# Hybrid vision block on one core: last states and the product with C on GpSimd, matmuls of an item ahead of the previous item's eviction, u * D summed in the turn

## The chip, the cores and the metric

The kernel runs on one core of a Trainium2 chip as a single launch. The core has five engines with a queue of instructions each: TensorE (PE, matrix products into PSUM; its weight loads are shown apart as PEld), VectorE (DVE), ScalarE (ACT), GpSimd (POOL) and SyncE (SP, which here only issues transfers). Each engine works through its own queue in order; an instruction that waits for another engine holds up all that stands behind it in its queue. The metric is the time of one execution on the device in microseconds (us), less is better. Device times given are medians of several runs; profiles are of one execution.

## The reference

Four images of 96 channels and 64 x 64 pixels go through four layers. Shortened to what is computed:

```python
# layer 0: x + conv(group_norm(x)); K=4 directions, N=16 states, DI=192 channels, L=4096 positions
u = silu(conv3x3_depthwise(Win @ gn(x)) + conv_b)              # b, 192, 64, 64
xs = [u by rows, u by columns, u by rows backwards, u by columns backwards]
dts, Bs, Cs = split(sel_w @ xs)                                # 6, 16, 16 rows for each direction
delta = softplus(dt_w @ dts + dt_b);  A = -exp(A_logs)
for t in range(L):                                             # a scan along the image
    h = h * exp(delta[t] * A) + (delta[t] * u[t]) * B[t]       # h: b, K, 192, 16
    y[t] = sum over the 16 states of h * C[t]
y = y + Ds * xs                                                # u * D
y = y0 + turned(y1) + y2 + turned(y3)                          # back to rows, summed
x = x + Wout @ layer_norm(y)
# layer 1: x + 1x1 conv to 576, relu, 3x3 depthwise conv, relu, 1x1 conv back to 96
# layer 2: t + ifft(relu(fft(relu(bn(W1 t))) * diag)) W2, then a feed-forward in quantised steps
# layer 3: t + linear attention (q k^T v without softmax), then a feed-forward
```

## The kernel before

**The scan and its slots.** The recurrence is the backbone. For each of the four images, four directions and eight chunks of 512 positions (128 steps in all) there are 12 units, and each unit takes one slot of the loop at L1228: 1536 slots. A unit holds 64 channels times 4 states as two halves of 128 partitions x 512. For each unit, `inputs` (L1141) makes db = (delta * u) * B for both halves at once on POOL, `decays` (L1145) makes exp(delta * A) on ACT into two PSUM banks, and `states` (L1155) runs two `tensor_tensor_scan` on DVE. In seven of the twelve units DVE also multiplies the states with C (L1166, result `hc`); in the other five, numbers 1, 3, 6, 8 and 10 (`POOL_C`), the scan writes to `hc` in SBUF and `product` (L1180) multiplies in place on POOL. `sums` (L1191) adds over the states with four small matmuls for two units, into bank `ps_y` (the trace has two records for each f32 matmul, so its counts on PE are twice those of the code); after the last pair of a group ACT copies the bank out (L1210).

**The state that is carried over.** `keep` (L1166 to L1178) saves the last column of every scan for the next chunk. For DVE's units ACT copies it from PSUM half by half (L1176); for POOL's units ACT copies both halves from `hc` (L1178), and since `product` overwrites `hc`, POOL waits for that copy.

**Order within a slot.** At slot s the loop issues: db of unit s+2, the kept states of unit s-1 together with the decays of unit s+1, POOL's product of unit s-1, the scans of unit s, the sums that are due, and then background work. The buffers `db` are three and `hc` five, the banks of decays four. Two units' sums fall due at the slot given at L1188: three slots after a POOL unit, two after another, the later of the two.

**Background.** All other layers are generators (streams) that yield before every piece of work the engine, an estimated time and the PSUM banks they need. Stages hold streams; `advance` (L1315) takes the next piece that fits from the streams of the first stage, `fits` (L1305) decides: a piece that depends on the stream's last piece on another engine is put in the same slot only after a PE piece, and only while this slot's PE estimate is at most 2.6 us; `ind` marks pieces that may go at once. `SHARE` caps each engine's background per slot, `rate` (L1238) the total. Stages run in the order of `plan` (L1076): front of images 1 and 2 (input convolution, delta, B, C), then for each image `turn` (L587: y of the two column directions is turned and added by PE), the convolutional layer, two `spectral` halves, `layer_2`, `layer_3`. Image 3's `turn` and convolution run as far as they get in the last eight steps, and the rest of image 3 runs alone after the scan, where all eight banks are used and every engine's queue is free of scan work. Three banks serve the background during the scan.

**Where u * D is added.** `scan_outputs` (L612) loads for each chunk u, the turned sum, y0 and y2, and adds them on PE: four matmuls for the first 128 channels (L638) and three, on stacked rows, for the rest (L649).

**The scheduler.** From slot 0 to the end of the scan the order of every engine is the order in which the code issues (L1351).

Of the kernel before, what the change touches and what calls it, by code (L numbers as in the profile page):

```python
# [10 lines left out]

# [16 lines left out]
L = H * W  # L28
# [22 lines left out]
WORK = {"weights": 47.0, "turn": 40.0, "front": 417.0, "conv": 468.0,  # L51
        "spectral": 111.2, "layer_2": 231.0, "product": 1.2, "layer_3": 153.6}
# [40 lines left out]
def hybrid_kernel(ctx: ExitStack, tc: tile.TileContext, a: dict):  # L93
# [347 lines left out]


# [95 lines left out]
    def scan_inputs(b, u, o, c, done):  # L538

        i = b % 3  # L540
        while not done.issuperset([c] if o == 0 else range(NCH)):
            yield wait(1)
# [12 lines left out]
        for part in range(3):  # L555
# [24 lines left out]
            yield ac(0.6, 0, True)  # L580
# [6 lines left out]
    def turn(b):  # L587
# [5 lines left out]
        for lo in (0, 128):  # L593
            for t, k in zip(parts, (1, 3)):
                load(t[:, :L].rearrange("p (c l) -> p c l", c=NCH),
                     d_y[k][im][:, lo : lo + 128, :].rearrange("c p l -> p c l"))
            yield wait(10)
            m, weights = (128, const("ident")) if lo == 0 else (64, const("two")[:, :64])
            for c in reversed(range(NCH)):
                yield pe(1.9, 1, True)  # L600
                p = bank()[:m]
                for n, t in enumerate(parts):
                    rhs = t[:, :L].rearrange("p (w h) -> p h w", h=H)[:, c * RPC : (c + 1) * RPC, :]
                    mm(split(p), lhsT=weights, rhs=rhs, start=n == 0, stop=n == 1)
                yield ac(0.6)
                s = tmp("yrow")[:m]
                nc.scalar.copy(s, p)
                free()
                later(d_yt[im][c][lo : lo + m], s)
            yield wait(2)  # L610

    def scan_outputs(b, done):  # L612

        parts = lambda c: [of[c] for of in (d_skip[b], d_yt[b % 2], d_y[0][b % 2], d_y[2][b % 2])]
        there = lambda c: scanned[b] >= 4 * NCH - c

        def fetch(*of):
            s = arrival("ypart")
            at = 0
            for x in of:  # L620
                load(s[at : at + x.shape[0]], x)
                at += x.shape[0]
            return s

        coming = None
        for c in reversed(range(NCH)):
            while not there(c):
                yield wait(1)
            if coming is None:
                coming = [fetch(of[:128]) for of in parts(c)]  # L630
                yield wait(3)
            whole, coming = coming, None
            yield pe(1.8, 1)
            p = bank()
            for n in range(4):
                if n == 2:
                    yield pe(1.8)
                mm(p, lhsT=const("ident") if n else skips[:, 0], rhs=whole[n], start=n == 0, stop=n == 3)  # L638
            yield ac(0.6)
            y = [tmp("yrow")]  # L640
            nc.scalar.copy(y[0], p)
            free()
            skip, yt, y0, y2 = parts(c)
            stacked = [fetch(skip[128:], yt[128:]), fetch(y0[128:]), fetch(y2[128:])]
            yield wait(2)
            yield pe(2.7, 1)
            p = bank()
            for n, s in enumerate(stacked):
                mm(p, lhsT=const("two") if n else skips[:, 1], rhs=s, start=n == 0, stop=n == 2)  # L649
            yield ac(0.6)  # L650
            y.append(tmp("yrow"))
            nc.scalar.copy(y[1], p)
            free()
            x = tmp("xc")
            load(x[:C], a["x"][b][:, chunk(c)])
            if c > 0 and there(c - 1):
                coming = [fetch(of[:128]) for of in parts(c - 1)]
# [36 lines left out]
    def conv_block(b):  # L694
# [6 lines left out]
        held = {}  # L701
        quads = [list(range(q, min(q + 4, NG))) for q in range(0, NG, 4)]
        slot = 0
# [14 lines left out]
        def hidden(xin, g, ready):  # L718
            nonlocal slot
            yield pe(0.9, 1, True)  # L720
            p = bank()
            for r in range(4):
                mm(p[32 * r : 32 * r + 32], lhsT=w1[:, 32 * g : 32 * g + 32], rhs=xin[:, r : r + 15 : 2, 1 : W + 1],  # L723
                   start=True, stop=True)
            yield ac(0.6)
            h = held["ring"][:, slot % 8]
            slot += 1
            act(h[:, :, 1 : W + 1], split(p), AF.Relu)
            free()
            ready.append(h)  # L730

        def rows(c):
            at = 6 * NG * 32
            xin = held["w"][:, at : at + 18 * (W + 2)].rearrange("p (r w) -> p r w", r=18)
            load(xin, d_x1[im][:, 16 * c : 16 * c + 18, :])
            yield wait(3)
            h2, ready = [], []
            for g in quads[0]:
                yield from hidden(xin, g, ready)
            for q, groups in enumerate(quads):  # L740
                coming = list(quads[q + 1]) if q + 1 < len(quads) else []
                here, ready = ready, []

                for out in ((0, 1) if len(groups) == 4 else (0,)):
                    where = [(i, out) for i in range(4)] if len(groups) == 4 else [(i, o) for o in (0, 1) for i in (0, 1)]
                    yield pe(2.7, 1, out > 0)
                    p = bank()
                    for dx in range(3):
                        for n, (i, o) in enumerate(where):
                            mm(p[32 * n : 32 * n + 32], lhsT=held["wd"][:, groups[i], o, dx, :],  # L750
                               rhs=here[i][:, :, dx : dx + W], start=dx == 0, stop=dx == 2)
                    yield ac(0.8)
# [4 lines left out]
                    for _ in range(2):  # L757
                        if coming:
                            yield from hidden(xin, coming.pop(0), ready)
            o = [tmp("o"), tmp("o")]  # L760
            for out in (0, 1):
# [14 lines left out]
                free()  # L776
            for half in (0, 1):
# [3 lines left out]
        done, to_norm = set(), []  # L781

        def blocks():
            yield from memory()
            for c in reversed(range(NCH // 2)):

                while max(2 * c - 1, 0) not in done:
# [717 lines left out]
```

## Time and profile before

| what | value |
|---|---|
| device time, median of 3 runs (lowest to highest) | 6944.3 us (6935.59 to 6944.92) |
| the profiled execution's own time, and its span | 6934.24 us, 6932.2 us |
| PE busy in the span | 4869.8 us (70%) |
| DVE busy | 5524.9 us (80%) |
| ACT busy | 4424.2 us (64%) |
| POOL busy | 5075.7 us (73%) |
| db on POOL (L1143) | 1536 of 2362 ns |
| product with C on POOL (L1181) | 640 of 2359 ns |
| decays on ACT (L1153) | 3072 of 691 ns |
| scans on DVE (L1162, four forms) | 3072 of 1204 to 1280 ns |
| product with C on DVE (L1166) | 1792 of 692 ns |
| kept state on ACT, DVE's units (L1176) / POOL's units (L1178) | 1568 of 157 ns / 560 of 185 ns |
| sums on PE (L1202) | 6144 records of 749 ns |
| transfers | 1121.47 MB, mean 162 GB/s |

The first scan starts at about 94 us and POOL's and PE's last scan work ends at about 6288 us; so the span falls into a short front, the scan, and a tail of 644 us. Read busy shares inside these stretches, not over the span: in the tail POOL has nothing to do. A waiting line is written "engine, what waited <- what it waited for"; the numbers behind it are us in total, how often, and the longest one.

### The profile page before, as it was taken

The numbers are of one execution on the slowest core, as the hardware profiler recorded it, in microseconds if no ns is written. First come the engines' busy times: TensorE is split into PE (matmuls) and PEld (weight loads), VectorE is DVE, ScalarE is ACT, GpSimd is POOL, SyncE is SP. The second block draws the span as 40 slices with busy tenths as digits, with TensorE's granted clock in tenths as the row PEclk, the third lists the DMA queues.
The fourth block names the chain that finished last, engine by engine and source line by source line (L and its number), as shares of the span: only waits on it lengthen the run. The fifth ranks groups of instructions, "written<-read, shape, count | busy, mean of one in ns | idle before, by whom it ended". The sixth has DMA issues, their size and how long they took to land. (4 is left out here: it accounts for less than half of the span.)

```text
span 6932.2 us, 85231 instructions
## 1 busy us (share of the span) xinstructions
PE 4869.8 (70%) x27820; PEld 1849.4 (27%) x27820; DVE 5524.9 (80%) x5803; ACT 4424.2 (64%) x8856; POOL 5075.7 (73%) x2183
## 2 busy tenths in 40 slices
PE   6623757656887766674688767666887676669986
PEld 2101212111224521220123353211234531112362
DVE  5979898888899889879899978998899788982110
ACT  5734776754576678776466557775565577753367
POOL 4756677678898888867899878898898788982000
PEclk9755978767998887886899877778998777779997
DMA  5544565566644544556664444456644444562030
GB/s 184 190 140 134 173 199 168 179 212 200 194 150 157 182 148 145 169 175 206 212 203 162 145 165 149 145 180 222 194 151 149 159 158 145 195 209 80 16 100 27
DMA packets 438832, 1121.47 MB, mean 162 GB/s; under 512 B 73002, under 2 KB 74768, under 8 KB 437140
## 3 DMA queue, kind: packets, MB, share of 16 engines
q1 hardware_dynamic: 438388, 1116.02, 49.0%
q8 instruction: 221, 3.62, 0.2%
q14 instruction: 223, 1.83, 0.1%
HBM read 881.28 MB, written 239.01 MB: 162 GB/s over the span
## 5 line engine op out<-in xcount | busy, mean ns | idle before, releaser
L1143 POOL TENSOR_TENSOR db<-rep_g,rep_BC 128x1024 f32<-128x1024 f32 x1536 | 3599.7, 2362 | 681.0 <-DVE hc L1162 190.5
L1153 ACT ACTIVATE ps_da<-rep_d,aneg 128x512 f32<-128x512 f32 x3072 | 2103.2, 691 | 458.0 <-DVE hc L1162 298.8
L1162 DVE TENSOR_TENSOR_SCAN ps_da<-ps_da,state,db 128x512 f32<-128x512 f32 x1568 | 2006.8, 1280 | 270.9 <-ACT state L1176 181.0
L1181 POOL TENSOR_TENSOR hc<-hc,rep_BC 128x1024 f32<-128x1024 f32 x640 | 1509.6, 2359 | 526.0 <-ACT state L1178 424.6
L1202 PE MATMUL ps_y<-hc,cst 128*32 128x512 f32 x6144 | 1045.7, 749 | 677.4 <-POOL hc L1181 556.9
L1162 DVE TENSOR_TENSOR_SCAN hc<-ps_da,state,db 128x512 f32<-128x512 f32 x1120 | 1371.1, 1266 | 108.2 <-ACT ps_da L1153 76.9
L1166 DVE TENSOR_TENSOR hc<-ps_da,rep_BC 128x512 f32<-128x512 f32 x1792 | 1239.3, 692 | 137.4 <-PE ps_y L1202 30.3
L1176 ACT COPY state<-ps_da 128x1 f32<-128x1 f32 x1568 | 246.3, 157 | 495.1 <-DVE hc L1166 494.4
L1202 PEld LDWEIGHTS ps_y<-hc,cst 128*32 128x32 f32 x6144 | 152.3, 119 | 1362.7 <-POOL hc L1181 849.9
L750 PE MATMUL ps_mm<-h,wd 128*32 128x512 f32 x3000 | 392.3, 597 | 10.1 <-ACT h L754 6.8
L510 PE MATMUL ps_mm<-xp,taps 128*128 128x512 f32 x576 | 295.6, 650 | 42.0 <-ACT xd L551 24.6
L1162 DVE TENSOR_TENSOR_SCAN ps_da<-ps_da,db 128x512 f32<-128x512 f32 x224 | 273.1, 1219 | 36.9 <-ACT state L1176 32.5
L723 PE MATMUL ps_mm<-wd,w 128*32 128x512 f32 x2000 | 280.1, 609 | 22.9 <-DMA wd<-x 8.9
L559 PE MATMUL ps_mm<-xd,dtw 128*128 128x512 f32 x256 | 180.1, 799 | 163.8 <-ACT z L581 127.6
L574 DVE SCALAR_TENSOR_TENSOR ps_mm<-ps_mm,z 128x512 f32<-128x512 f32 x192 | 133.1, 694 | 127.0 <-ACT state L1176 64.3
L1210 ACT COPY yt<-ps_y 128x512 f32<-128x512 f32 x256 | 149.1, 583 | 128.5 <-PE ps_y L1202 127.6
L546 PE MATMUL ps_mm<-ua,sel 128*128 128x512 f32 x128 | 118.3, 1018 | 157.6 <-ACT ua L529 100.6
L568 ACT ACTIVATE z<-ps_mm 128x512 f32<-128x512 f32 x192 | 114.9, 599 | 166.7 <-PE ps_mm L559 120.9
L581 ACT COPY z<-ps_mm 128x512 f32<-128x512 f32 x192 | 112.4, 585 | 166.5 <-DVE g L577 166.0
L1162 DVE TENSOR_TENSOR_SCAN hc<-ps_da,db 128x512 f32<-128x512 f32 x160 | 186.2, 1204 | 17.2 <-ACT ps_da L1153 17.2
L879 PE MATMUL ps_mm<-wa,xp 128*64 128x96 f32 x1728 | 135.0, 316 | 89.2 <-DVE d L882 72.6
L811 PE MATMUL ps_mm<-r,cst 128*128 128x512 f32 x206 | 142.8, 782 | 65.0 <-ACT r L808 19.3
(469 smaller groups left out, 7068.4 us busy)
## 6 DMA issues: line engine op xcount, KB each, us to landing
rep_BC<-bc SPq DMA_DIRECT2D x512, 512.0 KB
rep_g<-du SPq DMA_DIRECT2D x384, 512.0 KB
rep_d<-delta SPq DMA_DIRECT2D x384, 512.0 KB
y<-yt SPq DMA_DIRECT2D x512, 128.0 KB
du<-g SPq DMA_DIRECT2D x128, 256.0 KB
delta<-z SPq DMA_DIRECT2D x128, 256.0 KB
ypart<-y SPq DMA_DIRECT2D x128, 256.0 KB
tab<-in_etab SPq DMA_DIRECT2D x128, 256.0 KB
```

What stands on the lines that cost most here:

```text
L510: mm(p, lhsT=taps[:, t, 0:128], rhs=window(t, c + e), start=t == 0, stop=t == 8)
L559: mm(p, lhsT=dtw[:, o + 2 * part, 0:128], rhs=xd, start=True, stop=True)
L723: mm(p[32 * r : 32 * r + 32], lhsT=w1[:, 32 * g : 32 * g + 32], rhs=xin[:, r : r + 15 : 2, 1 : W + 1], start=True, stop=True)
L750: mm(p[32 * n : 32 * n + 32], lhsT=held["wd"][:, groups[i], o, dx, :], rhs=here[i][:, :, dx : dx + W], start=dx == 0, stop=dx == 2)
L1143: nc.gpsimd.tensor_mul(x["db"], x["step"]["g"][x["i"]], both(x["step"]["BC"][x["j"]][:, 0]))
L1153: act(x["da"][e], x["step"]["d"][x["i"]][:, e], AF.Exp, scale=aneg[:, av : av + 1])
L1162: nc.vector.tensor_tensor_scan(x["h"][e][:, order], x["da"][e][:, order], x["db"][:, e, order], start, ALU.mult, ALU.add)
L1166: x["made"] = nc.vector.tensor_mul(x["hc"][:, e], x["h"][e], x["step"]["BC"][x["j"]][:, 1])
L1176: nc.scalar.copy(to[:, e : e + 1], x["h"][e][:, end : end + 1])
L1181: x["made"] = nc.gpsimd.tensor_mul(x["hc"], x["hc"], both(x["step"]["BC"][x["j"]][:, 1]))
L1202: done = mm(y[32 * q : 32 * q + 32], lhsT=const("stack"), rhs=x["hc"][:, e], start=first or (x["pass"] == 0 and x["j"] == 0), stop=last or ...
L1210: nc.scalar.copy(yt, y)
```

## The change

Nine things are changed. (1) For POOL's units the last states are copied by POOL itself. (2) In a slot POOL's product comes ahead of db of the unit after next. (3) All sums fall due two slots after the pair's second unit. (4) `in_turn` issues the matmuls of an item before the eviction of the one before; `turn` and `spectral` use it, and the tables of `spectral` are loaded a part earlier. (5) `turn` also adds y0 and u * D, so `scan_outputs` adds two operands instead of four, both loaded one chunk ahead. (6) The first 1x1 convolution of layer 1 is a stream of its own that runs ahead of the depthwise part. (7) `turn` of images 2 and 3 runs as a stream beside `layer_3` of the image before. (8) `fits` lets only ACT follow PE in the same slot, up to 1.9 us of PE; the copy of delta waits a slot. (9) Four streams at once in front of images 1 to 3 and in the convolution; estimates in `WORK` follow.

```diff
-WORK = {"weights": 47.0, "turn": 40.0, "front": 417.0, "conv": 468.0,
-        "spectral": 111.2, "layer_2": 231.0, "product": 1.2, "layer_3": 153.6}
+WORK = {"weights": 47.0, "turn": 70.0, "front": 417.0, "conv": 447.0,
+        "spectral": 111.2, "layer_2": 231.0, "product": 1.2, "layer_3": 153.6, "layer_3_turn": 223.6}
...
+    def in_turn(items, make, matmuls, take, evict, depth=2):
+
+        made = []
+
+        def oldest():
+            p, item, at = made.pop(0)
+            yield take[:3] + (at,)
+            evict(p, item)
+            free()
+
+        for n, item in enumerate(items):
+            yield make[:3] + (n > 0,)
+            p = bank()
+            matmuls(p, item)
+            made.append((p, item, clock[0]))
+            if len(made) == depth:
+                yield from oldest()
+        while made:
+            yield from oldest()
...
-        while not done.issuperset([c] if o == 0 else range(NCH)):
-            yield wait(1)
+        if not done.issuperset([c] if o == 0 else range(NCH)):
+            while not done.issuperset([c] if o == 0 else range(NCH)):
+                yield wait(1)
+            yield wait(2)
...
-            yield ac(0.6, 0, True)
+            yield ac(0.6)
             nc.scalar.copy(z, p)
...
-            yield wait(10)
-            m, weights = (128, const("ident")) if lo == 0 else (64, const("two")[:, :64])
-            for c in reversed(range(NCH)):
-                yield pe(1.9, 1, True)
-                p = bank()[:m]
+
+            def fetch(c):
+                y, u = (t[:, L + c % 4 * CH : L + c % 4 * CH + CH] for t in parts)
+                load(y, d_y[0][im][c, lo : lo + 128])
+                load(u[: min(128, DI - lo)], d_skip[b][c, lo : min(lo + 128, DI)])
+                return y, u
+
+            whole = lo == 0
+            m, add = (128, const("ident")) if whole else (64, const("two")[:, :64])
+            skip = skips[:, 0] if whole else skips[:64, 1, :64]
+
+            def added(p, of):
+                c, (y, u) = of
+                p = p[:m]
                 for n, t in enumerate(parts):
                     rhs = t[:, :L].rearrange("p (w h) -> p h w", h=H)[:, c * RPC : (c + 1) * RPC, :]
-                    mm(split(p), lhsT=weights, rhs=rhs, start=n == 0, stop=n == 1)
-                yield ac(0.6)
+                    mm(split(p), lhsT=add, rhs=rhs, start=n == 0, stop=False)
+                mm(p, lhsT=add, rhs=y, start=False, stop=False)
+                mm(p, lhsT=skip, rhs=u[: skip.shape[0]], start=False, stop=True)
+
+            def stored(p, of):
                 s = tmp("yrow")[:m]
-                nc.scalar.copy(s, p)
-                free()
-                later(d_yt[im][c][lo : lo + m], s)
+                nc.scalar.copy(s, p[:m])
+                later(d_yt[im][of[0]][lo : lo + m], s)
+
+            chunks = ahead(1, fetch, reversed(range(NCH)))
+            first = next(chunks)
+            yield wait(10)
+            yield from in_turn(chain([first], chunks), pe(3.8, 1), added, ac(0.6), stored)
...
-        parts = lambda c: [of[c] for of in (d_skip[b], d_yt[b % 2], d_y[0][b % 2], d_y[2][b % 2])]
         there = lambda c: scanned[b] >= 4 * NCH - c
 
-        def fetch(*of):
-            s = arrival("ypart")
-            at = 0
-            for x in of:
-                load(s[at : at + x.shape[0]], x)
-                at += x.shape[0]
-            return s
+        def fetch(c):
+            out = []
+            for of in (d_yt[b % 2][c], d_y[2][b % 2][c]):
+                for part in (of[:128], of[128:]):
+                    s = arrival("ypart")
+                    load(s[: part.shape[0]], part)
+                    out.append(s[: part.shape[0]])
+            return out[0], out[2], out[1], out[3]
 
         coming = None
         for c in reversed(range(NCH)):
             while not there(c):
                 yield wait(1)
             if coming is None:
-                coming = [fetch(of[:128]) for of in parts(c)]
+                coming = fetch(c)
                 yield wait(3)
-            whole, coming = coming, None
-            yield pe(1.8, 1)
-            p = bank()
-            for n in range(4):
-                if n == 2:
-                    yield pe(1.8)
-                mm(p, lhsT=const("ident") if n else skips[:, 0], rhs=whole[n], start=n == 0, stop=n == 3)
-            yield ac(0.6)
-            y = [tmp("yrow")]
-            nc.scalar.copy(y[0], p)
-            free()
-            skip, yt, y0, y2 = parts(c)
-            stacked = [fetch(skip[128:], yt[128:]), fetch(y0[128:]), fetch(y2[128:])]
-            yield wait(2)
-            yield pe(2.7, 1)
-            p = bank()
-            for n, s in enumerate(stacked):
-                mm(p, lhsT=const("two") if n else skips[:, 1], rhs=s, start=n == 0, stop=n == 2)
-            yield ac(0.6)
-            y.append(tmp("yrow"))
-            nc.scalar.copy(y[1], p)
-            free()
+            parts, coming = coming, None
+            y = []
+            for name, of in (("ident", parts[:2]), ("two", parts[2:])):
+                yield pe(1.8, 1, name == "two")
+                p = bank()
+                for n, s in enumerate(of):
+                    mm(p, lhsT=const(name, slice(0, s.shape[0])), rhs=s, start=n == 0, stop=n == 1)
+                yield ac(0.6)
+                y.append(tmp("yrow"))
+                nc.scalar.copy(y[-1], p)
+                free()
             x = tmp("xc")
             load(x[:C], a["x"][b][:, chunk(c)])
             if c > 0 and there(c - 1):
-                coming = [fetch(of[:128]) for of in parts(c - 1)]
+                coming = fetch(c - 1)
...
+        def expansions():
+
+            yield from memory()
+            for c in reversed(range(NCH // 2)):
+
+                while max(2 * c - 1, 0) not in done or held.get("xin") is not None:
+                    yield wait(1)
+                at = 6 * NG * 32
+                xin = held["w"][:, at : at + 18 * (W + 2)].rearrange("p (r w) -> p r w", r=18)
+                load(xin, d_x1[im][:, 16 * c : 16 * c + 18, :])
+                held["xin"] = xin
+                yield wait(3)
+                for g in range(NG):
+                    while len(ready) - held["read"] == 8:
+                        yield wait(1)
...
+                first = held["read"]
+                while len(ready) < first + len(groups) or (ready[first + len(groups) - 1][1] == clock[0] and not alone):
+                    yield wait(1)
+                xin, here = held["xin"], [h for h, _ in ready[first : first + len(groups)]]
+
+                outs = (0, 1) if len(groups) == 4 else (0,)
...
-        return [Stage("conv", 3, norms(), scan_outputs(b, done), blocks())]
+        return [Stage("conv", 4, norms(), scan_outputs(b, done), blocks(), expansions())]
...
+        tables = ahead(2, lambda g: table("etab", g, 4), range(16))
+        first = next(tables)
+
+        z = big("z").rearrange("p (k h) -> p k h", k=64)
+        yield from in_turn(
+            range(C // 8), pe(0.7, 1), transform(d, "r1"), ac(1.1),
+            lambda p, g: nc.scalar.copy(z[:, :, g * 8 : g * 8 + 8], p.rearrange("p (h k) -> p k h", h=8)))
...
-            Stage("layer_3", 3, *(layer_3(c) for c in range(NCH))),
+            Stage("layer_3", 3, *(layer_3(c) for c in range(NCH))) if b not in (1, 2) else
+            Stage("layer_3_turn", 4, turn(b + 1), *(layer_3(c) for c in range(NCH))),
...
-        return [Stage("front", 3, *streams)]
+        return [Stage("front", 3 if b == 0 else 4, *streams)]
...
-        return [Stage("turn", 1, turn(b))] + conv_block(b)
+
+        return ([] if b >= 2 else [Stage("turn", 1, turn(b))]) + conv_block(b)
...
-                elif e == 1:
-                    nc.scalar.copy(to, x["hc"][:, :, end])
+                elif e == 0:
+                    nc.gpsimd.tensor_copy(to, x["hc"][:, :, end])
...
-            when = max(at - 1 + n + (3 if x["pool"] else 2) for n, x in enumerate(group))
+            when = at + 2
...
-            if slot + 2 < len(units):
-                inputs(units[slot + 2])
             if slot + 1 < len(units):
                 decays(units[slot + 1], units[slot - 1] if slot > 0 else None)
             if 0 < slot <= len(units):
                 if units[slot - 1]["pool"]:
                     product(units[slot - 1])
+            if slot + 2 < len(units):
+                inputs(units[slot + 2])
...
-
-        if not (ind or stream["was"] in ("wait", engine) or stream["at"] < clock[0]):
-            if stream["was"] != "pe" or tensor[0] > 2.6:
+        was, at = stream["was"], stream["at"]
+        if type(ind) is int:
+            ind, was, at = False, "pe", ind
+
+        if not (ind or was in ("wait", engine) or at < clock[0]):
+            if (was, engine) != ("pe", "act") or tensor[0] > 1.9:
```

## The prediction, made before the changed kernel ran

> **What bounds the kernel now.** First the stretches of the span: busy time of PE, weight loads, DVE, ACT and POOL, the granted clock, the share of the transfers.
>
> ```profile
> 94.00:6288.00 6194.00, 4258.90 (x23070) 1552.65 (x23074) 5433.06 (x5657) 4046.70 (x8260) 5058.65 (x2172) 0.80 0.52 173
> 6288.00:6932.00 644.00, 551.59 (x4582) 273.66 (x4574) 64.82 (x103) 337.20 (x533) 0.00 (x0) 0.92 0.17 51
> 6288.00:6545.00 257.00, 247.20 (x1500) 74.14 (x1492) 16.85 (x30) 87.09 (x135) 0.00 (x0) 0.99 0.15 40
> ```
>
> In the scan DVE is busy 88%, POOL 82%, PE 69%, ACT 65%. In the tail it is PE; in its first part, image 3's convolution, PE is busy 96%. A scan step of 12 slots takes 6194 / 128 = 48.4 us. DVE's own scan rows are 5077 us or 39.7 us a step, POOL's two rows 5109 us or 39.9 us. So two engines could run at about 42 us a step (DVE has 2.8 us of background), and 761 us of DVE idle in the scan are to be had. Second, whom DVE waits for in the scan, longest first:
>
> ```profile
> DVE ps_da L1162 <- ACT state L1176: 213.5, 115, 8.2
> DVE hc L1162 <- ACT ps_da L1153: 94.1, 38, 6.5
> DVE ps_mm L574 <- ACT state L1176: 64.3, 40, 5.1
> DVE st L461 <- DMA x<-in_x: 47.5, 5, 41.1
> DVE ps_da L1162 <- ACT state L1178: 38.1, 18, 5.7
> DVE hc L1166 <- PE ps_y L1202: 30.3, 17, 3.8
> DVE hc L1162 <- ACT state L1176: 28.6, 13, 8.0
> DVE ps_da L1162 <- POOL db L1143: 28.2, 19, 7.0
> ```
>
> It is ACT: with 23.1 us of one smaller row the scans wait 397 us for decays, and background pieces on DVE 102 us for ACT. POOL costs DVE only 28 us directly. But ACT is busy just 65%, so it is late because something stands in front of the decays in its queue. Third, therefore, what ACT, POOL and PE wait for in the scan:
>
> ```profile
> ACT z L581 <- DVE g L577: 163.8, 137, 3.5
> ACT yrow L607 <- PE ps_mm L604: 130.0, 56, 5.8
> ACT yt L1210 <- PE ps_y L1202: 127.3, 56, 10.1
> ACT z L568 <- PE ps_mm L559: 120.3, 47, 6.2
> ACT f L920 <- PE ps_mm L918: 78.0, 35, 8.2
> ACT y L948 <- PE ps_mm L946: 60.7, 39, 6.8
> ACT yrow L652 <- PE ps_mm L649: 44.2, 12, 6.0
> ```
>
> ```profile
> POOL hc L1181 <- ACT state L1178: 424.6, 192, 8.3
> ```
>
> ```profile
> PE ps_y L1202 <- POOL hc L1181: 556.9, 153, 17.8
> ```
>
> All of ACT's waits for background, its waits for a free decay bank left out, add up to some 1115 us. They close a ring: POOL's product waits 425 us for ACT's small copy, PE's sums wait 557 us for the product, background matmuls stand behind the sums, ACT stands in its evictions behind PE, and the decays stand behind ACT.
>
> **What the Trainium skill says.** "Perfetto Trace Analysis", Optimization Strategy: take the most-contended engine and look for what fills the gaps between its slices; that is the order above, and the trace agrees that DVE is that engine (88%). The same page, Optimizing Tensor Performance, wants independent matmul groups in different PSUM banks so that one is evacuated while the next is computed; that is what matmuls ahead of the eviction do, and rows like f, y and yrow show that it fails now. "GPSIMD Engine Reference", Performance versus the Vector engine, gives 2.6 cycles per element for two inputs, and "Trainium Kernel Development and Optimization", NeuronCore Architecture, 1.2 GHz: 1024 elements are an estimated 2.22 us. The trace has 2.36; the 0.14 us left are my estimate for the fixed price of a POOL instruction. And "GPSIMD Engine Reference", Instruction dispatch: completion gates only what waits on the instruction's semaphore. In the built order the product waits on the copy's own semaphore, so a wait is paid there too; no trace of before shows one such, POOL's products wait there for ACT.
>
> **The change part by part.** Sums are against the profiled execution's 6934.2 us.
>
> States and product on POOL. ACT loses 560 copies (103.5 us), POOL gets them. The trace of before has no such copy: below it is a 128x1 memset (0.10 us), above I allow 0.6 us for copy and own semaphore; I take 0.25 (0.14, and 0.1 for the wait: POOL starts 0.08 us after ACT's copy ends at 3007.23 us). 140 us fit into POOL's 1135 us of idle time, except where POOL is full (seven 200 us stretches with over 180 us of POOL work, 33 steps): 33 x 4.4 x 0.25 = +36; at 0.6 +87. The product moves ahead by one db, 2.36 us, and by the mean wait 424.6 / 560 = 0.76 us, less the copy: 2.9 us. Behind product and copy db comes later. Both need the end of the same scan (of the three buffers, the one db takes is freed by unit s-1), and DVE still has two slots to go, at least 6.5 us (two scans and two products of 1.27 and 0.69 us in one, two scans alone in the other), against 2.36 + 2.36 + 0.25 = 5.0 us: hidden, with 1.5 us to spare; a copy of over 1.5 us would make DVE wait for db.
>
> Sums two slots after the pair. Only pairs (0, 1) and (2, 3) move, one slot of 4.03 us forward; of the other four, three get their product 2.9 us earlier. `hc` comes free a slot sooner: of the 30 us of L1166 on `ps_y` I take 20 away.
>
> ACT behind PE and DVE. The copy of delta waits a slot (163.8), `turn` and `spectral` evict one item late (yrow 130.0, f 78.0, y 60.7, z 24.8), `scan_outputs` has its operands a chunk ahead (44.2 and 9.6), half of yt goes with the earlier product (63.7): 574.8 of 1115 us, 52%. I pass the share on to DVE's 397 + 102 us: -257. That step is a choice: DVE could lose all (-499) or, if ACT would have waited for its bank anyway, a small part (-60). What is late next is the softplus chain (z L568, untouched) and table loads.
>
> u * D in `turn`. Per chunk 12 matmuls replace 11: 32 more, 64 records of 0.6 us, 38 us on a PE with 69%: hidden, 38 if not. The same bytes are loaded, by SP, from `turn` instead of `scan_outputs`; two loads per item, one ahead, into four places: nothing waits behind them. PE's 119 us on ypart are gone, hidden in ACT's share.
>
> Stages. In the built order image 2's layer 3 ends at slot 1440 (before 1442), image 3's output sums begin at 1488 (1492) and its expansions at 1510 (1522). So more of image 3 lies inside the scan. In the tail remain 216 expansion matmuls (248), 324 depthwise ones (396), 4 output sums (21), 8 of the output norm (28). With two records each and 1.88 us for 16, 2.71 for 24 and 3.63 for 8: 7.5 + 16.3 + 15.4 + 18.2 = 57 us less of a PE that is 96% busy there; with tables loaded earlier, -60. A single stream with eight banks gains nothing from matmuls ahead of evictions. Expansions as a stream, four streams, the limit 1.9: order only, at nothing, +-40.
>
> Sum: -257 - 20 + 36 - 60 = -301, so 6633 us; the runs' median is 10 us above the profiled one: 6645 us.
>
> **The rivals.** *Deeper*: the ring is the only cause and nine tenths of ACT's lateness goes: -450 - 28 + 36 - 60, 6440 us. For it: the waits feed each other; against it: the front of images 0 to 2 takes 4.9 us a slot (94 to 1410 us: 271 slots, DVE busy 1114 us), and its table loads (1.28 us each) and softplus chain stay. *Shadow*: ACT's evictions wait while DVE is the bound anyway; DVE keeps its waits and gets 60 back, tail 40: 6845 us. For it: ACT waits 494 us for DVE's L1166, so it often stands where nothing is lost. *Slower*: the early sums stop PE. For pairs (0, 1) and (2, 3) they come 4.03 us earlier and their product 2.9 us: 1.16 us more waiting for 256 pairs, 297 us, at the point where the product is ahead by less than a slot; a dearer copy or a full POOL makes it worse. What ACT gains in its own waits it then loses to PE; passed on at the present rate of 499 to 1115, +133, with +36 and -60 that is 7053 us. For it: POOL is over 90% busy in the convolution and in parts of the spectral stage; against it, three pairs gain where two lose.
>
> **How the numbers follow.** This case 0.46 (own range 6550 to 6760), deeper 0.14, shadow 0.24, slower 0.13; 0.03 for no change within 0.2% (about what a measurement of this kernel can tell from none). Faster 0.84, slower 0.13. The range takes in shadow and the near half of deeper: 6440 to 6930, leaving out slower and the far half of deeper.
>
> **What would show it.** Right: L1181 waits only for DVE; the copy on POOL takes 0.1 to 0.3 us; L581, L607 and `spectral` rows leave ACT's waits; scans wait less than 250 us for ACT; DVE over 91% in the scan; the scan ends near 6050 us, the tail is near 585 us. Wrong: PE's wait for L1181 grows, DVE waits for db by 100 us and more, or copies of 0.6 us.

## The result and the profile after

| | before | after |
|---|---|---|
| device time, median (lowest to highest) | 6944.6 us (6935.6 to 6954.1) | 6704.2 us (6688.8 to 6708.9) |
| ratio to before, 95% interval | | 0.965, 0.9629 to 0.967 |
| profiled execution, span | 6934.2 us, 6932.2 us | 6708.9 us, 6707.1 us |
| end of the last scan on DVE | 6283.9 us | 6125.9 us |
| from there to the end of the span (tail) | 648.3 us | 581.2 us |
| DVE's waits in the scan, summed | 644 us | 485 us |
| of these, waits for ACT (scans and background) | 500 us | 344 us |
| ACT's own waits for PE, DVE and transfers in background work | 1112 us | 994 us |

The change saves 240 us by the medians. The two profiled spans differ by 225 us: 158 us in the scan and 67 us in the tail. The two stretches of the profile after, scan and tail; columns are length, busy time of PE, weight loads, DVE, ACT and POOL, granted clock, share of the transfers, GB/s:

```profile
89.00:6126.00 6037.00, 4291.33 (x23396) 1483.76 (x23392) 5435.38 (x5666) 4000.86 (x7732) 5156.80 (x2733) 0.82 0.55 178
6126.00:6707.00 581.00, 487.24 (x4332) 270.65 (x4324) 61.34 (x98) 320.01 (x507) 0.00 (x0) 0.91 0.17 49
```

DVE does the same work as before (5435 us) in a shorter scan; it is busy 90% of it. So the scan shortens by what DVE waits less, 644 - 485 = 159 us, and the question is where these waits went. One thing besides the order of work differs: the granted clock of TensorE in the scan is 0.82 where it was 0.80. No run holds it fixed, so its share of the gain isn't known. The records of the same sums took 746 ns on average instead of 749, so there it hardly shows. DVE's waits in the scan, after:

```profile
DVE ps_da L1197 <- ACT state L1211: 178.4, 98, 7.0
DVE ps_da L1197 <- POOL db L1178: 59.1, 65, 6.1
...
DVE ps_da L1197 <- ACT ps_da L1188: 34.1, 31, 4.4
...
DVE hc L1197 <- ACT ps_da L1188: 32.0, 21, 5.7
...
DVE hc L1197 <- PE ps_y L1237: 16.8, 3, 5.7
...
DVE hc L1201 <- PE ps_y L1237: 3.9, 3, 1.4
```

L1197 is the scan, L1188 the decays, L1211 ACT's copy of the last states. With their smaller rows, scans wait 267 us for ACT instead of 398, and more for db on POOL (L1178, 62 us instead of 29). The product (L1201) hardly waits for `ps_y` any more (30 before). ACT is still whom DVE waits for. What ACT waits for in its background work:

```profile
ACT yt L1245 <- PE ps_y L1237: 141.3, 68, 5.7
...
ACT yrow L642 <- PE ps_mm L638: 79.5, 36, 4.9
ACT xd L574 <- PE ps_mm L570: 77.1, 30, 3.9
ACT yrow L680 <- PE ps_mm L677: 66.3, 37, 5.6
...
ACT z L604 <- DVE g L600: 4.9, 9, 1.0
```

One line has gone: the copy of delta (L604) waited 164 us for DVE and waits 5. The evictions have not: `turn` (L642) waits 79.5 us where it waited 130, but yt waits longer (127 before), xd waits 77 (10 before) and `scan_outputs` (L680) 66 (54 before, in two lines). All of ACT's background waits for PE add up to 967 us after and 935 before. POOL and PE in the scan:

```profile
POOL state L1213 <- DVE hc L1197: 294.2, 202, 38.8
POOL db L1178 <- DMA rep_BC<-bc: 276.7, 83, 11.0
...
PE ps_y L1237 <- POOL hc L1216: 348.2, 99, 11.9
PE ps_y L1237 <- DVE hc L1201: 236.4, 77, 43.3
```

POOL no longer waits for ACT (425 us before). It waits for the scan itself instead, and longer for the rows of B and C (176 before). PE waits 348 us for POOL's product, 557 before, and 236 for DVE's, 78 before. POOL's order in the scan, by the timeline (start, duration, instruction, idle time ahead of it and what ended that):

```profile
3002.77 0.19 POOL L1213 COPY state<-hc 128x2 f32<-128x2 f32 x1 [2.20 <-DVE hc L1197]
3003.04 2.36 POOL L1216 TENSOR_TENSOR hc<-hc,rep_BC 128x1024 f32<-128x1024 f32 x1
3005.36 2.36 POOL L1178 TENSOR_TENSOR db<-rep_g,rep_BC 128x1024 f32<-128x1024 f32 x1
```

The copy takes 0.19 us, and the product starts 0.08 us after its end.

### The profile page after: what moved, and what is told of

Same layout as the page of the kernel before. It is cut to its first block, busy times and chain, and to the rows that moved or that the text cites. A ratio compares the mean times of both kernels' runs of the same rounds, so it can differ in the third digit from the quotient of the medians.

```text
span 6707.1 us, 84452 instructions
## 1 busy us (share of the span) xinstructions
PE 4836.7 (72%) x27884; PEld 1777.4 (26%) x27884; DVE 5521.4 (82%) x5803; ACT 4357.4 (65%) x8296; POOL 5173.5 (77%) x2743
## 5 line engine op out<-in xcount | busy, mean ns | idle before, releaser
L1178 POOL TENSOR_TENSOR db<-rep_g,rep_BC 128x1024 f32<-128x1024 f32 x1536 | 3600.2, 2364 | 551.0 <-DMA rep_BC<-bc 281.9
L1188 ACT ACTIVATE ps_da<-rep_d,aneg 128x512 f32<-128x512 f32 x3072 | 2067.3, 690 | 542.0 <-DVE hc L1197 404.5
L1197 DVE TENSOR_TENSOR_SCAN ps_da<-ps_da,state,db 128x512 f32<-128x512 f32 x1568 | 2007.1, 1280 | 237.3 <-ACT state L1211 154.5
L1237 PE MATMUL ps_y<-hc,cst 128*32 128x512 f32 x6144 | 1026.7, 746 | 619.3 <-POOL hc L1216 348.2
L1197 DVE TENSOR_TENSOR_SCAN hc<-ps_da,state,db 128x512 f32<-128x512 f32 x1120 | 1371.1, 1266 | 70.3 <-ACT ps_da L1188 23.1
L1201 DVE TENSOR_TENSOR hc<-ps_da,rep_BC 128x512 f32<-128x512 f32 x1792 | 1239.2, 692 | 112.5 <-PE ps_y L1237 3.9
L1211 ACT COPY state<-ps_da 128x1 f32<-128x1 f32 x1568 | 247.2, 158 | 471.1 <-DVE hc L1201 466.3
L786 PE MATMUL ps_mm<-h,wd 128*32 128x512 f32 x3048 | 348.5, 593 | 7.0 <-ACT r L153 7.0
L1213 POOL COPY state<-hc 128x2 f32<-128x2 f32 x560 | 106.0, 189 | 306.9 <-DVE hc L1197 294.2
L1197 DVE TENSOR_TENSOR_SCAN ps_da<-ps_da,db 128x512 f32<-128x512 f32 x224 | 273.6, 1221 | 41.7 <-ACT state L1211 23.8
L763 PE MATMUL ps_mm<-wd,w 128*32 128x512 f32 x2032 | 261.2, 621 | 36.8 <-DMA wd<-x 11.9
L1197 DVE TENSOR_TENSOR_SCAN hc<-ps_da,db 128x512 f32<-128x512 f32 x160 | 186.2, 1204 | 9.4 <-ACT ps_da L1188 9.0
L569 PE MATMUL ps_mm<-ua,sel 128*128 128x512 f32 x128 | 101.3, 880 | 114.7 <-ACT z L604 91.1
(420 smaller groups left out, 6954.1 us busy)
```

The source lines that it names most:

```text
L763: mm(p[32 * n : 32 * n + 32], lhsT=w1[:, 32 * g : 32 * g + 32], rhs=xin[:, n : n + 15 : 2, 1 : W + 1], start=True, stop=True)
L1178: nc.gpsimd.tensor_mul(x["db"], x["step"]["g"][x["i"]], both(x["step"]["BC"][x["j"]][:, 0]))
L1188: act(x["da"][e], x["step"]["d"][x["i"]][:, e], AF.Exp, scale=aneg[:, av : av + 1])
L1197: nc.vector.tensor_tensor_scan(x["h"][e][:, order], x["da"][e][:, order], x["db"][:, e, order], start, ALU.mult, ALU.add)
L1201: x["made"] = nc.vector.tensor_mul(x["hc"][:, e], x["h"][e], x["step"]["BC"][x["j"]][:, 1])
L1211: nc.scalar.copy(to[:, e : e + 1], x["h"][e][:, end : end + 1])
```

## The experiments

Two theories stood against each other. *Ring*: the prediction's own, in which POOL's wait for ACT's copy closes the circle, so that the three POOL parts (1, 2 and 3 of the change) carry much of the gain. *Evictions*: ACT is late because it stands in its own background waits, for DVE (the copy of delta) and for PE; POOL's wait lies beside the path. All runs in one table, times in us; "scan end" is the end of the last scan on DVE, the tail is what follows, and both, like the waits, come from the profiled execution. The runs come from several rounds, in which the median of the kernel before lay between 6938.7 and 6944.6 us, so a difference of two medians from different rounds is uncertain by some 6 us.

| run | median | ratio to before, 95% interval | scan end | tail | DVE's waits, of these for ACT |
|---|---|---|---|---|---|
| e1_pool_parts | 6944.1 | 1.0011 (1.0004 to 1.0018) | 6286 | 647 | 649, 490 |
| e2_without_pool_parts | 6717.8 | 0.9685 (0.967 to 0.9699) | 6130 | 578 | 481, 349 |
| e3_copy_alone | 6932.9 | 0.9991 (0.9983 to 1.0) | 6272 | 645 | 633, 469 |
| e6_delta_copy_waits | 6854.1 | 0.9883 (0.9868 to 0.9898) | 6146 | 706 | 511, 368 |
| e7_delta_copy_at_once | 6747.8 | 0.9725 (0.9711 to 0.974) | 6165 | 580 | 517, 378 |
| e8_turn_by_itself | 6818.6 | 0.9833 (0.9818 to 0.9847) | 6125 | 706 | 486, 332 |
| e9_both | 6899.7 | 0.9938 (0.9919 to 0.9957) | 6196 | 709 | 564, 398 |
| e10_evict_at_once | 6791.7 | 0.9791 (0.9777 to 0.9806) | 6159 | 634 | 513, 414 |
| e11_sums_out_later | 6663.0 | 0.9595 (0.9579 to 0.9611) | 6082 | 583 | 449, 348 |
| e14_sums_later_on_before | 6939.7 | 1.0002 (0.9992 to 1.0012) | 6278 | 647 | 640, 471 |
| e16_all_but_pool_later | 6691.0 | 0.9642 (0.9623 to 0.9661) | 6113 | 581 | 467, 345 |
| e17_limit_2_6 | 6677.4 | 0.9622 (0.9601 to 0.9643) | 6109 | 582 | 464, 392 |

**The POOL parts, alone and left out.** On the kernel before, first the copy of the states alone (e3), then all three parts (e1):

```diff
-                elif e == 1:
-                    nc.scalar.copy(to, x["hc"][:, :, end])
+                elif e == 0:
+                    nc.gpsimd.tensor_copy(to, x["hc"][:, :, end])
...
-            when = max(at - 1 + n + (3 if x["pool"] else 2) for n, x in enumerate(group))
+            when = at + 2
...
-            if slot + 2 < len(units):
-                inputs(units[slot + 2])
             if slot + 1 < len(units):
                 decays(units[slot + 1], units[slot - 1] if slot > 0 else None)
             if 0 < slot <= len(units):
                 if units[slot - 1]["pool"]:
                     product(units[slot - 1])
+            if slot + 2 < len(units):
+                inputs(units[slot + 2])
```

> The kernel before, only the last states of POOL's units are copied by POOL. Ring theory: the product comes 0.76 us sooner, less 0.25 us for the copy; 20 to 60 us, 6885 to 6925 us. Eviction theory: nothing, 6930 to 6960 us. Price theory: the copy delays db, which stands behind nothing it can hide under, and DVE waits for db by over 60 us (28 before): 6960 us or more.

> The kernel before with the three POOL parts alone: last states copied by POOL, product ahead of db, sums two slots after the pair. Ring theory (POOL's wait for ACT's copy goes on through the product, PE's sums, ACT's evictions and the decays to DVE): 50 to 110 us of the scan go, 6835 to 6895 us, POOL's product no longer waits for ACT (425 us before), PE waits under 450 us for the product (557 before). Eviction theory (ACT stands in its own background evictions, POOL is not on the path): 6925 to 6965 us. Early sums theory (PE stops at sums that come a slot sooner): over 6965 us.

The copy alone is worth 0.1% by its ratio (0 to 0.17%); all three parts together gain nothing and are 0.1% slower. In the trace of e1 the parts do what they should, and DVE hardly notices:

```profile
POOL state L1178 <- DVE hc L1162: 334.5, 219, 41.3
POOL db L1143 <- DVE ps_da L1162: 295.0, 142, 8.3
...
DVE ps_da L1162 <- ACT state L1176: 184.0, 111, 8.3
DVE hc L1162 <- ACT ps_da L1153: 85.6, 36, 6.4
DVE ps_da L1162 <- ACT ps_da L1153: 65.1, 39, 8.3
```

The 425 us in which POOL's product waited for ACT are gone. In their place POOL waits for the next scan, ahead of the copy and of db: it was early, it is earlier now, and it waits for DVE all the same. DVE's waits for ACT are 490 us instead of 500. e1 also issues the sums of two pairs a slot early: PE's wait for POOL's product falls from 557 to 446 us, and its wait for DVE's products (L1166) grows from 78 to 246. So e1 alone can't tell an idle link from a gain that the early sums took back. e3 leaves the sums where they were; POOL's wait for ACT is gone there too, yet PE still waits 542 us for the product. The product ahead of db without the early sums was not tried. The other side, the changed kernel with the three parts undone (the diff above backwards):

> The changed kernel with the three POOL parts undone; all background parts stay. Ring theory: 6760 to 6810 us, the tail as short as in the changed kernel (576 us) and the scan 50 to 110 us longer. Eviction theory: within 25 us of the changed kernel, 6690 to 6730 us. If the two halves add up, what e1 gains and what e2 loses against the changed kernel are equal within 20 us.

It is 14 us slower by the medians, and its scan ends 4 us later. That is within what the evictions theory expected, as e1 and e3 are. The ring falls: the wait that I took for its closing link was slack, that is, POOL lost no time in it that it wouldn't have lost to the next wait.

**The copy of delta.** On the kernel before, this alone (e6); and the changed kernel with this alone taken back (e7):

```diff
-            yield ac(0.6, 0, True)
+            yield ac(0.6)
             nc.scalar.copy(z, p)
```

> The kernel before, only the copy of delta out of PSUM waits for the next slot, so that ACT no longer stops for DVE's multiplication (164 us before). Eviction theory, with the share of the prediction (499 of 1115 us reach DVE): 74 us less, 6855 to 6890 us. Ring theory: that wait lies beside DVE's own work, at most 25 us, 6920 to 6945 us.

> The changed kernel, but the copy of delta may go in the slot of DVE's multiplication again, as before. If that piece is worth the same on either side (85 us alone on the kernel before): 6770 to 6800 us, ACT waits about 160 us for DVE's g again (7 us in the changed kernel). If the other background parts had already taken the same time: under 6730 us.

DVE's and ACT's waits in the scan of e6; before they were 213.5, 94.1, 64.3 and 163.8 us:

```profile
DVE ps_da L1162 <- ACT state L1176: 166.7, 117, 5.5
DVE hc L1162 <- ACT ps_da L1153: 82.2, 46, 5.1
...
DVE ps_mm L574 <- ACT state L1176: 39.3, 26, 5.4
...
ACT z L581 <- DVE g L577: 9.1, 14, 1.0
```

One word in one line takes 138 us off the scan of the kernel before and 85 us off the time, at the edge of what the evictions theory expected: DVE's waits for ACT fall from 500 to 368 us, while ACT's wait for DVE in this line falls from 164 us to 9. That fits the evictions theory: the copy stood at the head of ACT's queue for an operand that DVE was just making, and the decays that DVE needed next stood behind it.

Two things limit this reading. First, these copies run only until about 3257 us, in the first half of the scan. The 768th slot's scans end at 3364 us before and at 3272 us in e6, 92 us earlier, and DVE waits 88 us less up to there. The other 46 us come in the second half, where no such copy runs. What differs there is that later stages lie some 20 slots later, and why that saves time stays open. Second, the gains don't add up, and both expectations for e7 are missed. Without the delta copy's wait the other parts still bring the scan end to 6165 us, 119 us earlier than before, and with it to 6126, only 39 more. At the middle they nearly add: 92 us by the delta copy, 48 by the other parts, 113 by both (3364 us before, 3316 in e7, 3251 after). Most of what is missing, 72 of 99 us, is missing in the second half, where no copy of delta runs; why is open as well.

In e6 the tail grows by 58 us. These are the depthwise matmuls of image 3's convolution that are left after the scan, first in e6, then in the kernel before, in two of three banks; the numbers are count, shortest, median and longest in ns, first and last start:

```profile
L750 PE MATMUL ps_da<-h,wd x480: 590/592/617, 6189.8 to 6454.7; 128*32 128x512 f32 x160
L750 PE MATMUL ps_mm<-h,wd x312: 590/592/617, 6180.5 to 6457.3; 128*32 128x512 f32 x156
```

```profile
L750 PE MATMUL ps_da<-h,wd x360: 590/592/617, 6312.5 to 6534.5; 128*32 128x512 f32 x180
L750 PE MATMUL ps_mm<-h,wd x336: 590/592/617, 6292.2 to 6531.9; 128*32 128x512 f32 x168
```

With the third bank there are 864 records in e6 and 792 before. In e6 they run until 311 us after the scan, before until 251 us after it. A piece that waits a slot makes its stream longer in slots. Counted in the traces by the decays that stand ahead of it on ACT, the last copy of image 2's layer 3 comes in slot 1476 in e6 instead of 1456, and all of image 3's expansions and depthwise matmuls fall behind the scan. That this work has moved out is hardly what shortens the scan: e8 below moves more of it out, and its scan ends as it did.

**Turn beside layer 3.** The changed kernel, with `turn` of images 2 and 3 as a stage by itself again:

```diff
-            Stage("layer_3", 3, *(layer_3(c) for c in range(NCH))) if b not in (1, 2) else
-            Stage("layer_3_turn", 4, turn(b + 1), *(layer_3(c) for c in range(NCH))),
+            Stage("layer_3", 3, *(layer_3(c) for c in range(NCH))),
...
-        return ([] if b >= 2 else [Stage("turn", 1, turn(b))]) + conv_block(b)
+        return [Stage("turn", 1, turn(b))] + conv_block(b)
```

> The changed kernel, but the turns of images 2 and 3 are stages of their own again instead of streams beside layer 3. Placement theory: the last image's output sums start some slots later and more of its convolution falls into the tail, 20 to 50 us, 6725 to 6755 us, with a longer tail than 576 us. Rival, that the turn costs its slots wherever it stands: within 10 us of the changed kernel.

The scan ends as it did (6125 us), the tail is 125 us longer. That is more than twice what either expectation allows for. Layer 3 of image 2 ends in slot 1485 instead of 1456, by the same count, and the expansions and depthwise matmuls of image 3 all fall behind the scan: 288 of the code's expansion matmuls and 432 depthwise ones instead of 220 and 336. So part 7 is worth 114 us by the medians, all in the tail; it pays for the slots that the delta copy costs.

**Matmuls ahead of the eviction.** The changed kernel with each item evicted before the next one's matmuls:

```diff
-    def in_turn(items, make, matmuls, take, evict, depth=2):
+    def in_turn(items, make, matmuls, take, evict, depth=1):
```

> The changed kernel with a depth of one in in_turn: turn and spectral evict each item before the matmuls of the next, as before. Eviction theory: ACT's waits for the turn's and the spectral matmuls come back to about 290 us (185 in the changed kernel), at the rate of the delta copy (85 us for 164) that is 40 to 70 us, 6745 to 6775 us. Rival, that waits for PE are not lost as waits for DVE are, since DVE works on meanwhile: within 15 us of the changed kernel.

It costs 87 us, more than expected: 33 in the scan, where ACT's background waits for PE grow from 967 to 1022 us and DVE's waits for ACT from 344 to 414 us, and 52 in the tail (layer 3 of image 2 ends in slot 1501). The granted clock in the scan is 0.80 here too, against 0.82.

**Sums out a slot later.** A try of my own on what is left after: yt is ACT's longest background wait, and SP's store of yt stands behind it in SP's queue, ahead of the loads that POOL waits for. The copy, the store and the count are put off to the slot after the last sums, ahead of that slot's sums:

```diff
             if last:
-                yt = sp.tile([128, CH], F32, name="yt")
-                nc.scalar.copy(yt, y)
...
+                summed.append((step, group[0]["pass"], y))
...
+        def sums_out():
+            while summed:
+                step, part, y = summed.pop(0)
+                yt = sp.tile([128, CH], F32, name="yt")
+                nc.scalar.copy(yt, y)
...
+            sums_out()
             for group in due.get(slot, ()):
                 sums(group)
```

> The changed kernel, and ACT's copy of the sums out of PSUM is issued in the slot after the last sums instead of right behind them, the store and the count of finished steps with it. Eviction theory: ACT's 145 us of waiting for the sums go, 30 to 75 us less, 6630 to 6675 us. Rival: ACT's waits for PE cost DVE nothing: within 15 us of the changed kernel.

This is faster than both kernels, by 41 us than the changed one. DVE, POOL, PE and SP's queue in its scan:

```profile
DVE ps_da L1197 <- POOL db L1178: 15.1, 15, 4.7
...
POOL db L1178 <- DMA rep_BC<-bc: 36.9, 11, 8.3
...
PE ps_y L1237 <- ACT yt L1252: 151.5, 34, 10.1
...
SPq L433 <- ACT yt L1252: 385.5, 87, 14.8
```

SP stands 386 us in the store of yt instead of 658, POOL's wait for the rows of B and C falls from 277 to 37 us, scans wait 16 us for db instead of 62. PE pays 152 us of waiting for the bank. The expectation named another way: ACT's wait for the sums does go (141 to 8 us), but DVE's waits for ACT stay as they were (344 and 348 us). DVE waits 36 us less in all, and its scans 46 us less for db, so the gain came by way of db. That the loads came sooner because the store moved is read from SP's wait; the copy, the store and the count were not moved one by one. The same edit on the kernel before (e14), and on the changed kernel without the POOL parts (e16):

> The kernel before, with ACT's copy of the sums, its store and its count issued a slot after the last sums. Standing theory (ACT is late because it stands in its own waits, and the store that waits for ACT holds up SP's later loads): ACT's 127 us of waiting for ps_y and a large part of POOL's 181 us for rep_BC go, 20 to 60 us less than before, about 6900 us. Rival (the 41 us that the same edit took from the changed kernel hang on POOL being ahead there, with 282 us of waiting for rep_BC): within 15 us of before.

> The changed kernel with the sums out later, and with the three POOL parts taken back (state copy on ACT, product after db, sums due a slot later for two pairs). Theory that the POOL parts are worth nothing by themselves: within 15 us of the run with the sums out later (6663 us), so 6650 to 6680. Rival (the POOL parts were only hidden by the wait for rep_BC, which the later sums take away): they are worth their 103 us of ACT, 30 us and more, so 6695 us or above.

On the kernel before it is worth nothing, though SP's wait for yt falls there too (688 to 413 us): POOL's wait for these rows stays (176 and 160 us), and POOL waits 404 us for ACT's copy. So a shorter stay of SP in that store isn't enough by itself. Without the POOL parts it is worth 27 us (e2 to e16), with them 41 (after to e11); e16 lies between its two expectations. Seen the other way, the POOL parts are worth 14 us in the changed kernel and 28 us once the sums go out later. The two edits work on two waits of POOL: in e16 it waits 325 us for ACT's copy and 138 us for the rows, in e11 0 and 38.

**The POOL parts beside the delta copy, and the limit.** The kernel before with e1's and e6's edits (e9); and e11 with the old limit:

```diff
-            if (was, engine) != ("pe", "act") or tensor[0] > 1.9:
+            if (was, engine) != ("pe", "act") or tensor[0] > 2.6:
```

> The kernel before with the copy of delta waiting a slot and the three POOL parts, nothing else. If POOL's parts are worth nothing also once ACT no longer waits for DVE: within 15 us of the delta copy alone (6854 us). Rival, that they need ACT's queue free to show their gain: 30 us or more below it, 6825 us or less.

> The changed kernel with the sums out later, and the limit on PE's work ahead of an eviction in the same slot at its old 2.6 instead of 1.9. Theory of ACT standing behind PE: more evictions close behind their matmuls, ACT's waits for PE grow by 100 us or more and 10 to 40 us come back in the scan; layer 3 of image 2 ends 8 slots sooner and no matmul of image 3 moves out of the tail. Rival (the limit does nothing, the delta copy and the early matmuls did it all): within 10 us of 6663 us.

In e9 neither expectation holds: with the POOL parts the kernel of e6 becomes 46 us slower, all of it in the scan. PE's waits for the sums' operands, e6 and then e9:

```profile
PE ps_y L1202 <- POOL hc L1181: 525.3, 144, 13.7
PE ps_y L1202 <- DVE hc L1166: 118.7, 29, 41.1
```

```profile
PE ps_y L1202 <- POOL hc L1181: 439.2, 125, 13.0
PE ps_y L1202 <- DVE hc L1166: 305.4, 85, 42.6
```

The earlier sums get POOL's product 86 us less late and DVE's 187 us later. DVE's background waits 28 us more for ACT and 19 us more for PE, its scans 23 us more for POOL. That fits a PE that stands in sums issued too early; the due time was not tried by itself there. Another reading is open: the granted clock in the scan is 0.80 against 0.81 in e6, and a record of the sums takes 758 ns on average against 734. With the old limit (e17) the time is 14 us longer than in e11, which is little beside the spread of the runs (6668 to 6693 us against 6646 to 6667): ACT's background waits for PE grow by 51 us and DVE's waits for ACT by 44.

## Why the prediction was right, and where it was not

The time and the sign held: 6704 us against 6645, inside the range, which from 6440 to 6930 takes in almost any gain. (Its last step, 6633 plus 10, makes 6643.) The way there did not hold: for the scan the terms came to -241 us where 158 went. That the sum came as near as it did is in part luck.

- **-257 us, ACT behind PE and DVE.** This is the term that failed, in both of its steps. The first said that 574.8 of ACT's 1115 us of waits go; 118 went. The delta copy's 164 did go, but evictions wait for PE as long as before (935 and 967 us). From e7 to the changed kernel the delta copy's wait falls by 157 us and the waits for PE grow by 89, from 878 to 967 (yt 100 to 141, `xd` 50 to 77, softplus row 73 to 105); from before to e6, with the same edit, they fall from 935 to 883. So waits were passed on in the one kernel and not in the other, and why stays open. The second step passed ACT's share on to DVE in proportion. Instead DVE's waits for ACT fell by 156 us, more than ACT's own waits did. The length of a wait did not tell its worth: e6 removes a line of 164 us and gains 85 us of time, e1 removes one of 425 and gains nothing. Of the scan's 158 us, taking single parts back from the changed kernel costs 39 (delta copy), 33 (early matmuls) and 4 (POOL parts); what earns the rest was not found.
- **The ring.** Its link POOL to ACT was slack, by e1, e2 and e3. e6 and e10 point to ACT's own queue instead.
- **-20 us, `ps_y`.** This held: DVE's products wait 4 us for it instead of 30, and 28 again without the POOL parts (e2). Scans that write into `hc` now wait 17 us for the sums to release it, but they do so in e2 as well (17 us), so this isn't the price of the early sums.
- **+36 us, copies on POOL.** The copy's price held: copy and wait take 0.27 us where 0.25 was taken. "GPSIMD Engine Reference", Instruction dispatch, says that completion gates only what waits on the semaphore; the product that waits for the copy starts 0.08 us after it. That scans wait 33 us more for db (62 instead of 29) fits the term only by luck: with the copy alone (e3) they wait 29 us as before, and in e11, which keeps all copies but hardly waits for the rows of B and C, 16 us.
- **-60 us, the tail.** 67 us. The mechanism held as well: in the traces image 3's expansions start in slot 1511 instead of 1525, and 220 of them and 336 depthwise matmuls are left after the scan, where 216 and 324 were foretold. e8, e10 and e6 each move layer 3 of image 2 to a later slot, and the tail grows by 52 to 125 us.
- **u * D in `turn`, at nothing.** No run had it alone. PE's background waits for transfers fell from 234 to 102 us, 119 of them being the wait on ypart. This may be part of the 119 us that the scan gains in e7; which of the parts that remain there earn them stays open. Taking all slot rules back together was not tried.
- **The rivals.** *Slower* did not come about in the changed kernel: PE waits 606 us for the sums' operands, 661 before. But the POOL parts do lengthen this wait wherever they are added: from 661 to 708 us in e1, 694 to 759 in e9, 596 to 606 from e2 to the changed kernel. *Shadow* gave DVE back 60 us of waiting, and 159 came back; *deeper* took away nine tenths of the waits for ACT, and 156 of 500 us went.
- **What would show it.** As foretold: POOL's product waits almost only for DVE, copies of 0.19 us, the tail at 576 us by the measure used there. Missed: scans wait 267 us for ACT (below 250), `turn` still waits 79.5 us for PE, DVE is busy 90% (over 91%), the scan ends at 6131 us by that measure (6050). None of the signs of being wrong came: PE's wait for POOL's product fell, DVE waits 62 us for db, a copy takes 0.19 us. They could not tell that the ring was wrong; e1 to e3 could.

## What to carry to other kernels

Price a wait by what stands behind it in the queue of the engine that waits, and by whether the bottleneck needs that next; a long wait on an engine that must wait for the bottleneck anyway is worth nothing. Gains of edits made together need not add: try each alone and each left out before sharing a gain among them, and compare at a point in the middle too, to see where a gain comes from. When a piece of work is made to wait for its slot, count what it pushes past the end of the overlapped part, since it comes back in the tail.

## What the runs showed of the hardware

Nothing of a single instruction's cost was far from what was taken; a small copy on POOL (128x2) takes 0.19 us, hardly more than ACT needed for the same (0.185 us). Not expected was how far a store may reach. In the changed kernel SP stands 658 us in the store of yt, which waits for ACT, and POOL waits 277 us for loads that SP issues. Moving copy and store by a slot (e11) brought this to 386 and 37 us and took 41 us off the time. It isn't a rule of its own: the same edit on the kernel before (e14) took 275 us off SP's wait, 16 us off POOL's, and nothing off the time.
